# A selective-scan kernel on one core: the work of two state groups put into one GpSimd product

## The chip, the cores and the metric

The kernel runs on one core of a Trainium2 chip. The core has a matrix engine (TensorE, PE in the profile), three engines for elementwise work (VectorE is DVE, ScalarE is ACT, GpSimd is POOL), and SyncE (SP), which here only issues DMAs. Each engine takes its instructions strictly in the order of its own queue and waits on semaphores for the others. The metric is the device time of one execution in microseconds; less is better.

## The reference

Layer 0 is a ConvNeXt block (7x7 depthwise convolution, norm over channels, two dense products with GELU, residual) on x of 32 x 96 x 56 x 56. Layer 1 is two Mamba blocks over the 3,136 positions of each image, then a global-pool branch, a 1x1 fusion and a batch norm with residual. The part that matters here is the selective scan of a Mamba block, with 192 inner channels and 16 states for each:

```python
dbl = xc @ xproj_w
dt = dbl[..., :DTRANK]
Bm = dbl[..., DTRANK:DTRANK + DSTATE]
Cm = dbl[..., DTRANK + DSTATE:]
delta = jax.nn.softplus(dt @ dt_w + dt_b)
A = -jnp.exp(A_log)
dA = jnp.exp(delta[..., None] * A)
dBx = delta[..., None] * Bm[:, :, None, :] * xc[..., None]
# h[t] = dA[t] * h[t-1] + dBx[t]
hstates = jax.lax.associative_scan(comb, (dA, dBx), axis=1)[1]
y = jnp.einsum('blds,bls->bld', hstates, Cm) + Dp * xc
y = y * jax.nn.silu(z)
```

## The kernel before, in words

**Set-up.** The convolution of the first 12 images, the weights and layer 0 of the first image come first (about 0.8 ms). At the end, about 0.35 ms, the batch norm is applied to stored results.

**Stages and steps.** Everything between is a sequence of 256 stages: 32 images x 4 chunks of 784 positions x 2 Mamba blocks, the two blocks taken in turn. A stage has 24 steps, numbered n = 4j + g. A step is one scan on 128 partitions: 32 channels (j = 0 to 5) by 4 states (g = 0 to 3). "Step 24" below is step 0 of the next stage.

**What a step is made of.**
- ACT writes the factor dA (`exps`, L890), into PSUM where g = 3 or j is 2 or 5, else into a "da" tile in SBUF.
- For j = 0, 1, 3, 4, PE spreads delta*xc over the four states (`spread`, L905), once for each j, and DVE multiplies it by B (`times_b`, L878): two products ahead of the scan of g = 0 and two ahead of that of g = 1. For j = 2 and 5 (`POOLED`) GpSimd makes these products (`pooled`, L915) from a copy "us" that came by DMA.
- DVE scans (`tensor_tensor_scan`, L938) into a ring of 4 states of 784 columns.
- GpSimd multiplies the state by C (L942) into the da tile, and PE adds the four states of a channel into the PSUM tile y (`add_up`, L975), three steps later in program order.
- When both j of a pair are added up, DVE multiplies y by silu(z) (`gate`, L956). y has one buffer, so the next pair's first matmul (L969) waits for the gate. Gates stand at steps 4 and 12, and behind step 19.

**What runs beside it.** The stage's own queue positions also carry the preparation of the next stage (`prep`), the end of the last one (`post`), half a chunk of layer 0 for a later image (`block0`) and, in 192 of the stages, one channel pair of the convolution (`conv`). The order is written out by hand: each piece has a slot number, whole part the step behind which it is put into the queues, fraction the order within it; a scheduler does not move anything. Slots that the prediction speaks of: at step 0 the last part of the input projection (`project(2, wx, ...)`, L633, 16 matmul passes of PE), at step 1 silu(xc) and the projection for z (12 passes) with silu(z) (L646), which loads an activation table before it and one behind it; the layer 0 norm `hz` on DVE ahead of step 14 and the two `hn` products ahead of step 15; convolution taps at steps 7 to 10 and 18 to 22 (L552). In step n ACT's exp of step n+1 (if it goes to PSUM) and of n+2 (if to SBUF) is queued ahead of the scan. GpSimd's u = delta*xc (L712) stands at slot 16.9, its last third at 25.2.

**Queues.** `pooled` for j = 2 stands behind steps 0, 2, 4, 6, for j = 5 behind steps 12, 14, 16, 18. All loads and stores of the stages go through SP in program order: B and C of a group in one tile "bc" (8 buffers, loaded at slots 10.2 and 13.2), delta (L742), u out and back in as "us" (L726, L733), x for two stages at once (L420).

Of the kernel before, what the change touches and what calls it, by code (L numbers as in the profile page):

```python
# [34 lines left out]
F32 = mybir.dt.float32  # L35
I32 = mybir.dt.int32
AF = mybir.ActivationFunctionType
ALU = mybir.AluOpType
# [23 lines left out]
def convnext_mamba_kernel(  # L62
# [211 lines left out]
    for i in range(2):  # L274
        d = {}
        lg, lb = column(ln_g[i], C, f"lg{i}"), column(ln_b[i], C, f"lb{i}")
        wz = const.tile([C + 1, 2 * DIN], F32, name=f"inw{i}", tag=f"inw{i}")
        norm_weights(wz, in_w[i], lg, lb)
        wx = const.tile([C + 1, 4, DIN], F32, name=f"wx{i}", tag=f"wx{i}")
        nc.gpsimd.dma_start(wx, taps[i].partition_broadcast(C + 1))  # L280
        for k in range(4):
            nc.vector.tensor_tensor(wx[:, k, :], wx[:, k, :], wz[:, 0:DIN], ALU.mult)
        d["wx"], d["wz"] = wx, wz[:, DIN : 2 * DIN]
        d["cb"] = blocks(mconv_b[i], f"cb{i}")
# [59 lines left out]
    with ExitStack() as main:  # L344
# [7 lines left out]
        def work(shape, name, bufs):  # L352

            pool, n = (pre[0], 3) if pre else (wp, bufs)
            return pool.tile(shape, F32, name=name, tag=name, bufs=n)
# [41 lines left out]
        batch_sums = {}  # L397
        xins = {}

        def block0(b, c, s):  # L400
# [16 lines left out]
            def load_x():  # L417
                if s == 0:
                    xins[b, c] = work([C, CH], "xin", 1)
                    nc.sync.dma_start(xins[b, c], x[b, :, c * CH : (c + 1) * CH])  # L420

# [35 lines left out]
            def down():  # L457
                v["ps"] = psum(2)
                nc.tensor.matmul(
                    v["ps"][0:C, 0:HC], eye, xins[b, c][:, tok(s)], start=True, stop=False  # L460
                )
                for f in range(NF):
                    nc.tensor.matmul(
                        v["ps"][0:C, 0:HC], w2_sb[:, f, :], v["gl"][:, f, :],
                        start=False, stop=(f == NF - 1),
                    )

            def residual():
                xs = xins[b, c][:, tok(s)]
                nc.scalar.activation(  # L470
                    xs, v["ps"][0:C, 0:HC], AF.Identity, bias=b2ls,
                    accum_out=batch_sums[b][:, k : k + 1],
                )
                if s == 1:
                    nc.sync.dma_start(x1_d[b][:, c * CH : (c + 1) * CH], xins.pop((b, c)))

# [110 lines left out]
        def prep(S):  # L587
# [77 lines left out]
            def dbl_out():  # L665
                v["dbl"] = wp.tile([NX, CH], F32, name="dbl", tag="dbl", bufs=1)
                for a in range(2):
                    nc.scalar.copy(v["dbl"][:, tok(a)], v["pss"][a][0:NX, 0:HC])  # L668
                v["bd"] = bcd.tile([2 * NS, CH], F32, name="bd", tag="bd")
                nc.sync.dma_start(v["bd"], v["dbl"][DTR:NX, :])  # L670
                S.bcs = []

            def load_bc(gs):
                def piece():
                    for g in gs:
                        t = wp.tile([128, 2, CH], F32, name="bc", tag="bc", bufs=8)
                        for k in range(2):
                            src = v["bd"][NS * k + 4 * g : NS * k + 4 * g + 4, :]
                            nc.sync.dma_start(
                                t[:, k, :], src.unsqueeze(0).broadcast_to([32, 4, CH])  # L680
                            )
                        S.bcs.append(t)

                return piece
# [22 lines left out]

            def product(lo, hi):
                def piece():
                    if lo == 0:  # L710
                        S.u = wp.tile([128, NQ, HC], F32, name="u", tag="u", bufs=1)
                    nc.gpsimd.tensor_tensor(  # L712
                        S.u[:, lo:hi], v["dl"][:, lo:hi], S.xc[:, lo:hi], ALU.mult
                    )

                return piece

# [42 lines left out]
            elif S is stages[3]:  # L760
# [13 lines left out]
                (t[6] + 0.2, silu("z", None)), (t[7], dbl), (t[8], dbl_out),  # L774
                (max(10.2, t[8] + 1.2), load_bc((0, 1))), (max(13.2, t[8] + 2.2), load_bc((2, 3))),
                (t[9], dt), (t[10], softplus),
                (max(16.9, t[10] + 1.5), product(0, 2)), (max(18.3, t[10] + 3.1), store_u(0)),
                (25.2, product(2, 3)), (26.3, store_u(1)),
                (max(17, t[10] + 2), load_d4(0)), (max(18, t[10] + 3), load_d4(1)),
# [66 lines left out]

        ring = wp.tile([128, NG, CH], F32, name="h", tag="h", bufs=1)
        LAG = 3
        LATE = (4, 12)

# [21 lines left out]

        def product_tile(S, j, g):
            t = S.da[j, g] = wp.tile([128, CH], F32, name="da", tag="da", bufs=11)
            return t

        def times_b(S, out, g):
            nc.vector.tensor_tensor(  # L878
                halves(out), S.u4.rearrange("p (a b) -> p a b", a=2)[:, :, 0:HC],
                halves(S.bcs[g][:, 0, :]), ALU.mult,  # L880
            )

        def exps(n):

            m, r = divmod(n, NSTEP)
            if m == len(stages):
                return
            S, j, g = stages[m], r // NG, r % NG
            e = wide(g % 2)[:, 0:CH] if in_psum(j, g) else product_tile(S, j, g)
            nc.scalar.activation(e, S.d4[j], AF.Exp, scale=S.d["A"][:, j, g : g + 1])  # L890
            S.e[j, g] = e
# [17 lines left out]

        def pooled(m, j, g):  # L910


            def piece():
                S = stages[m]
                nc.gpsimd.tensor_tensor(  # L915
                    product_tile(S, j, g), S.us[j], S.bcs[g][:, 0, :], ALU.mult
                )

            return piece

        def scan(n):
            m, r = divmod(n, NSTEP)
            S, j, g = stages[m], r // NG, r % NG
            d, c = S.d, S.c
            if r in LATE and n >= NSTEP // 3:
                gate(n - LAG - 2)
            run(n, within)
            if j not in POOLED and g < 2:
                if g == 0:
                    S.w = wide(1)[:, 0:CH]  # L930
                times_b(S, S.w, g)
                if g == 0:
                    times_b(S, product_tile(S, j, NG - 1), NG - 1)
                else:
                    times_b(S, S.u4[:, 0:CH], 2)
            da = S.da[j, g]
            db = da if in_psum(j, g) else S.u4[:, 0:CH] if g == 2 else S.w
            nc.vector.tensor_tensor_scan(  # L938
                ring[:, g, :], S.e.pop((j, g)), db, 0.0 if c == 0 else d["st"][:, j, g : g + 1],
                ALU.mult, ALU.add,  # L940
            )
            nc.gpsimd.tensor_tensor(da, ring[:, g, :], S.bcs[g][:, 1, :], ALU.mult)  # L942

        def keep_state(n):

            m, r = divmod(n, NSTEP)
            S, j, g = stages[m], r // NG, r % NG
            if g % 2 == 1 and S.c < NCH - 1:
                nc.scalar.copy(  # L949
                    S.d["st"][:, j, g - 1 : g + 1].unsqueeze(2), ring[:, g - 1 : g + 1, CH - 1 : CH]  # L950
                )
# [6 lines left out]
        def add_up(n):  # L958

            if n < 0:  # L960
                return
            m, r = divmod(n, NSTEP)
            S, j, g = stages[m], r // NG, r % NG
            q = j // 2
            if j % 2 == 0 and g == 0:
                if j == 4:
                    gate(n - 1)
                S.y = py.tile([128, 512], F32, name="y", tag="y")
                nc.tensor.matmul(  # L969
                    S.y[:, 0:HC], S.d["D"][:, q, :], S.xc[:, q, :], start=True, stop=False  # L970
                )
            da = S.da.pop((j, g))
            for a in range(2):
                r0 = 64 * a + 32 * (j % 2)
                nc.tensor.matmul(  # L975
                    S.y[r0 : r0 + 32, 0:HC], ssum, da[:, tok(a)],
                    start=False, stop=(g == NG - 1),
                )
# [18 lines left out]
        for m, S in enumerate(stages):  # L997
            if m:
                put(m, post(stages[m - 1]))
            for j in POOLED:  # L1000
                put(m, [(NG * (j - 2) + 2 * g, pooled(m, j, g)) for g in range(NG)])
            if 2 <= m < len(halfs) + 2:
# [8 lines left out]
        with tc.manual_schedule(  # L1011
# [9 lines left out]
            for n in range(end + NSTEP):  # L1021
# [9 lines left out]
                if n < end + LAG:  # L1031
                    if n % NSTEP in LATE:
                        add_up(n - LAG - 1)
                    if n % NSTEP + 1 not in LATE:
                        add_up(n - LAG)
                elif n == end + LAG:
                    gate(end - 1)
# [100 lines left out]
```

## Time and profile before

| what | value |
|---|---|
| median of 3 runs | 16963.9 us (16960.82 to 16972.59) |
| the profiled execution, its span | 16951.94 us, 16950.2 us |
| PE, DVE, ACT, POOL busy | 90%, 92%, 68%, 92% of the span |
| stages from 2,000 to 15,000 us | 208 pairs of the two u products (L712): 62.5 us a stage |
| distance of two u products between 8,000 and 8,070 us | 61.24 us (8006.49 to 8067.73) |
| granted PE clock, 2,000 to 15,000 us | 0.96 |
| DMA engines | 42% busy, 138 GB/s, 2,000 to 15,000 us |

Every row of the profile tells the number of instructions, their busy time, the mean duration of one, and the idle time of the engine just ahead of them with what ended it. Where instructions follow each other without a wait, the distance of two starts in the timeline is what one costs its queue; it is a little less than the duration, since one starts before the last has ended.

### The profile page before, as it was taken

How to read it: one execution, taken by the hardware profiler on the slowest of the kernel's cores; microseconds unless marked ns; L12 is line 12 of the kernel's file. 1: busy time of each engine (PE TensorE's matmuls, PEld its weight loads, DVE VectorE, ACT ScalarE, POOL GpSimd, SP SyncE). 2: the span in 40 equal slices, each digit the busy share in tenths (PEclk: the TensorE clock that was granted, in tenths of full speed). 3: DMA queues.
4: the chain of work that ended last, by engine and by line, in shares of the span. 5: the costliest groups of instructions: out<-in, count | busy, mean ns of one | idle time of the engine just before them, and what ended most of it. 6: DMA issues, size and time to landing. Idle time of an engine off the chain costs nothing. (4 is left out here: it accounts for less than half of the span.)

```text
span 16950.2 us, 206740 instructions
## 1 busy us (share of the span) xinstructions
PE 15327.0 (90%) x69336; PEld 5507.9 (32%) x69336; DVE 15667.8 (92%) x12351; ACT 11444.5 (68%) x18723; POOL 15657.7 (92%) x8798
## 2 busy tenths in 40 slices
PE   8899999999999999999999999999998888888881
PEld 5333333333333333333333333333332222222220
DVE  8699999999999999999999999999999999999994
ACT  1577777777777777777777777677776777676653
POOL 1699999999999999999999999999999999999991
PEclk9899999999999999999999999999999999999985
DMA  4344444444444444444444444444443433433338
GB/s 113 109 139 142 142 135 140 139 142 141 135 142 140 142 135 140 142 141 137 138 141 141 142 134 141 140 143 137 137 142 131 133 126 129 134 132 133 125 121 280
DMA packets 1303109, 2362.11 MB, mean 139 GB/s; under 512 B 516398, under 2 KB 669242, under 8 KB 1302040
## 3 DMA queue, kind: packets, MB, share of 16 engines
q1 hardware_dynamic: 1292712, 2308.46, 42.0%
q10 hardware_dynamic: 7168, 38.54, 0.6%
q8 instruction: 546, 8.95, 0.2%
q14 instruction: 523, 4.28, 0.1%
q0 software_dynamic: 2160, 1.88, 0.1%
HBM read 1945.97 MB, written 402.41 MB: 139 GB/s over the span
## 5 line engine op out<-in xcount | busy, mean ns | idle before, releaser
L942 POOL TENSOR_TENSOR da<-h,bc 128x784 f32<-128x784 f32 x6144 | 11296.0, 1864 | 428.7 <-DVE h L938 356.3
L975 PE MATMUL y<-da,ssum 128*32 128x392 f32 x24576 | 5193.2, 547 | 232.7 <-POOL da L942 229.1
L890 ACT ACTIVATE w<-d,A 128x784 f32<-128x784 f32 x3072 | 2810.9, 916 | 2442.6 <-DVE h L938 2403.6
L938 DVE TENSOR_TENSOR_SCAN h<-w,st,da 128x784 f32<-128x784 f32 x2304 | 4120.7, 1831 | 267.6 <-ACT w L890 261.5
L938 DVE TENSOR_TENSOR_SCAN h<-da,st,w 128x784 f32<-128x784 f32 x2304 | 4176.3, 1834 | 3.6 <-ACT st L949 3.2
L915 POOL TENSOR_TENSOR da<-us,bc 128x784 f32<-128x784 f32 x2048 | 3811.8, 1861 | 0.0
L878 DVE TENSOR_TENSOR w<-w,bc 128x784 f32<-128x784 f32 x3072 | 2910.6, 978 | 325.6 <-PE w L905 257.4
L890 ACT ACTIVATE da<-d,A 128x784 f32<-128x784 f32 x3072 | 2834.6, 939 | 19.0 <-DMA d<-dd 16.0
L633 PE MATMUL ps<-hn,wx 97*64 97x392 f32 x12288 | 2263.2, 503 | 11.0 <-DVE hn L621 11.0
L975 PEld LDWEIGHTS y<-da,ssum 128*32 128x32 f32 x24576 | 1079.4, 116 | 3366.9 <-issue 2015.7
L905 PE MATMUL w<-u,sel 64*128 64x392 f32 x4096 | 992.4, 560 | 555.8 <-DVE h L938 436.8
L938 DVE TENSOR_TENSOR_SCAN h<-w,da 128x784 f32<-128x784 f32 x768 | 1327.4, 1771 | 125.6 <-ACT w L890 118.0
L938 DVE TENSOR_TENSOR_SCAN h<-da,w 128x784 f32<-128x784 f32 x768 | 1345.4, 1773 | 0.0
L633 PEld LDWEIGHTS ps<-hn,wx 97*64 97x64 f32 x12288 | 797.5, 136 | 1422.4 <-issue 1113.2
L712 POOL TENSOR_TENSOR u<-dl,xc 128x784 f32<-128x784 f32 (+1 forms) x512 | 736.9, 1439 | 471.0 <-ACT dl L698 471.0
L552 PE MATMUL ps<-xpad,band 112*112 112x168 f32 (+1 forms) x5376 | 1086.6, 312 | 0.0
L552 PEld LDWEIGHTS ps<-xpad,band 112*112 112x112 f32 x5376 | 709.8, 175 | 1088.3 <-issue 972.7
L690 PE MATMUL ps<-dbl,dtw 6*64 6x392 f32 x3072 | 728.0, 536 | 310.9 <-ACT dbl L668 310.9
L878 DVE TENSOR_TENSOR da<-w,bc 128x784 f32<-128x784 f32 x1024 | 988.0, 965 | 1.0 <-DMA bc<-bd 1.0
L368 ACT ACT_TABLE_LOAD x759 | 973.8, 1283 | 14.2 <-PEq L1125 0.8
L377 ACT ACTIVATE sq<-ps 96x392 f32<-96x392 f32 x768 | 345.1, 490 | 759.9 <-PE ps L372 343.6
L969 PE MATMUL y<-xc,D 128*128 128x392 f32 x1536 | 790.3, 601 | 32.8 <-DVE z L956 32.8
(152 smaller groups left out, 14579.4 us busy)
## 6 DMA issues: line engine op xcount, KB each, us to landing
bc<-bd SPq DMA_DIRECT2D x2048, 392.0 KB, 6.5
d<-dd SPq DMA_DIRECT2D x1536, 392.0 KB, 3.6
us<-uu SPq DMA_DIRECT2D x512, 392.0 KB, 3.3
dd<-dl SPq DMA_DIRECT2D x512, 294.0 KB, 3.7
band<-band_d SPq DMA_DIRECT2D x192, 343.0 KB, 4.3
uu<-u SPq DMA_DIRECT2D x1024, 49.0 KB, 3.0
cv<-conv_d SPq DMA_DIRECT2D x256, 147.0 KB, 3.4
xin<-in_x SPq DMA_DIRECT2D x128, 294.0 KB, 3.9
```

Of the source, the lines that this page charges most:

```text
L368: nc.scalar.preload_act_table_set("natural_log_exp_and_others")
L552: nc.tensor.matmul(v["ps"][0:R2, 0 : (last - first) * W], v["band"][:, dw, :], xpad[:, first:last, dw : dw + W], start=(dw == 0), stop=(dw ...
L633: nc.tensor.matmul(v["x", q][rows(a), 0:HC], weights[:, k, 64 * q : 64 * q + 64], v["hn"][:, o : o + HC], start=(k == 0), stop=(k == last),)
L712: nc.gpsimd.tensor_tensor(S.u[:, lo:hi], v["dl"][:, lo:hi], S.xc[:, lo:hi], ALU.mult)
L878: nc.vector.tensor_tensor(halves(out), S.u4.rearrange("p (a b) -> p a b", a=2)[:, :, 0:HC], halves(S.bcs[g][:, 0, :]), ALU.mult,)
L890: nc.scalar.activation(e, S.d4[j], AF.Exp, scale=S.d["A"][:, j, g : g + 1])
L905: nc.tensor.matmul(S.u4[:, 512 * a : 512 * a + HC], sel[rows(a), j % 2, :], S.u[rows(a), j // 2, :], start=True, stop=True,)
L915: nc.gpsimd.tensor_tensor(product_tile(S, j, g), S.us[j], S.bcs[g][:, 0, :], ALU.mult)
L938: nc.vector.tensor_tensor_scan(ring[:, g, :], S.e.pop((j, g)), db, 0.0 if c == 0 else d["st"][:, j, g : g + 1], ALU.mult, ALU.add,)
L942: nc.gpsimd.tensor_tensor(da, ring[:, g, :], S.bcs[g][:, 1, :], ALU.mult)
L969: nc.tensor.matmul(S.y[:, 0:HC], S.d["D"][:, q, :], S.xc[:, q, :], start=True, stop=False)
L975: nc.tensor.matmul(S.y[r0 : r0 + 32, 0:HC], ssum, da[:, tok(a)], start=False, stop=(g == NG - 1),)
```

## The change

- The product with C is made once for two scans: one GpSimd instruction over 2 x 784 columns, queued behind the scan of odd g. The ring of states has 6 places instead of 4.
- `pooled` also makes two groups at once, with the copy "us" read twice: behind steps 1 and 5 for j = 2, behind 13 and 17 for j = 5.
- The da tiles become pairs: 6 of 2 x 784 columns instead of 11 of 784. B and C get tiles of their own, each for two groups: three B pairs and four C pairs. B and C of groups 0 and 1 are loaded at slot 10.2, C of groups 2 and 3 at 13.2, B of these at 18.3.
- `add_up` is queued for two steps at a time, at even steps (steps 0 and 1 at step 4, and so on). The gates stand ahead of steps 4, 12 and 20.
- u is one product of 1,176 columns at slot 16.9; x is loaded and stored by halves of a chunk; the constant tile of the input weights keeps the half for z alone, which costs one copy for each block in the set-up.

```diff
-            if r in LATE and n >= NSTEP // 3:
+            if r in GATES and n >= NSTEP // 3:
                 gate(n - LAG - 2)
...
-            nc.gpsimd.tensor_tensor(da, ring[:, g, :], S.bcs[g][:, 1, :], ALU.mult)
+            if g % 2 == 1:
+                k = (n - 1) % NR
+                nc.gpsimd.tensor_tensor(da, ring[:, k : k + 2, :], S.bc[1, g // 2], ALU.mult)
...
                 nc.gpsimd.tensor_tensor(
-                    product_tile(S, j, g), S.us[j], S.bcs[g][:, 0, :], ALU.mult
+                    pair(S, j, h), S.us[j].unsqueeze(1).broadcast_to([128, 2, CH]), S.bc[0, h],
+                    ALU.mult,
                 )
...
-                put(m, [(NG * (j - 2) + 2 * g, pooled(m, j, g)) for g in range(NG)])
+                put(m, [(NG * (j - 2) + 4 * h + 1, pooled(m, j, h)) for h in range(2)])
...
                 if n < end + LAG:
-                    if n % NSTEP in LATE:
+                    if (n - LAG) % 2 == 1:
                         add_up(n - LAG - 1)
-                    if n % NSTEP + 1 not in LATE:
                         add_up(n - LAG)
...
-                if j == 4:
-                    gate(n - 1)
...
-        ring = wp.tile([128, NG, CH], F32, name="h", tag="h", bufs=1)
+        NR = 6
+        ring = wp.tile([128, NR, CH], F32, name="h", tag="h", bufs=1)
         LAG = 3
-        LATE = (4, 12)
+        GATES = (4, 12, 20)
...
+        def pair(S, j, h):
+
+            if (j, h) not in S.da:
+                S.da[j, h] = wp.tile([128, 2, CH], F32, name="da", tag="da", bufs=6)
+            return S.da[j, h]
...
-                (max(10.2, t[8] + 1.2), load_bc((0, 1))), (max(13.2, t[8] + 2.2), load_bc((2, 3))),
+                (max(10.2, t[8] + 1.2), load_bc(0, 0)), (max(10.2, t[8] + 1.2), load_bc(1, 0)),
+                (max(13.2, t[8] + 2.2), load_bc(1, 1)), (max(18.3, t[8] + 2.2), load_bc(0, 1)),
                 (t[9], dt), (t[10], softplus),
-                (max(16.9, t[10] + 1.5), product(0, 2)), (max(18.3, t[10] + 3.1), store_u(0)),
-                (25.2, product(2, 3)), (26.3, store_u(1)),
+                (max(16.9, t[10] + 1.5), product), (max(18.5, t[10] + 3.1), store_u(0)),
+                (26.3, store_u(1)),
...
-                    xins[b, c] = work([C, CH], "xin", 1)
-                    nc.sync.dma_start(xins[b, c], x[b, :, c * CH : (c + 1) * CH])
+                v["xin"] = work([C, HC], "xin", 1)
+                nc.sync.dma_start(v["xin"], x[b, :, k * HC : (k + 1) * HC])
```

## The prediction

> **What bounds the kernel now.** First the page: shares of busy time, then the product with C.
>
> ```profile
> PE 15327.0 (90%) x69336; PEld 5507.9 (32%) x69336; DVE 15667.8 (92%) x12351; ACT 11444.5 (68%) x18723; POOL 15657.7 (92%) x8798
> ...
> L942 POOL TENSOR_TENSOR da<-h,bc 128x784 f32<-128x784 f32 x6144 | 11296.0, 1864 | 428.7 <-DVE h L938 356.3
> ```
>
> Three engines stand at 90% or more, so no single one is "the bound"; a stage takes 62.5 us because three queues hand work to each other. The list of waits of the whole span shows where they lose it:
>
> ```profile
> DVE h L938 <- ACT w L890: 379.5, 264, 4.6
> POOL da L942 <- DVE h L938: 356.3, 476, 20.5
> DVE w L878 <- PE w L905: 257.4, 281, 8.9
> DVE z L956 <- PE y L975: 109.6, 107, 5.0
> ```
>
> DVE waits for ACT's exp and for PE's spread, GpSimd seldom for DVE, the gate hardly ever. To see what is behind "ACT w" I took the timelines of one stage. PE:
>
> ```profile
> 8018.15 0.85 PE L975 MATMUL y<-da,ssum 128*32 128x392 f32 x4
> 8019.27 0.85 PE L975 MATMUL y<-da,ssum 128*32 128x392 f32 x4 [0.28 <-POOL da L942]
> 8020.06 2.86 PE L633 MATMUL ps<-hn,wx 97*64 97x392 f32 x16
> 8022.84 0.85 PE L975 MATMUL y<-da,ssum 128*32 128x392 f32 x4
> 8023.63 2.20 PE L633 MATMUL ps<-hn,inw 97*64 97x392 f32 x12
> 8025.76 0.85 PE L975 MATMUL y<-da,ssum 128*32 128x392 f32 x4
> ```
>
> ACT, and DVE's scan of step 3:
>
> ```profile
> 8025.87 0.50 ACT L646 ACTIVATE z<-ps 128x392 f32<-128x392 f32 x1 [0.16 <-PE ps L633]
> 8026.39 1.28 ACT L368 ACT_TABLE_LOAD   x1
> 8027.68 0.92 ACT L890 ACTIVATE w<-d,A 128x784 f32<-128x784 f32 x1
> ```
>
> ```profile
> 8028.70 1.79 DVE L938 TENSOR_TENSOR_SCAN h<-w,da 128x784 f32<-128x784 f32 x1 [1.63 <-ACT w L890]
> ```
>
> The reader is to see a chain: a GpSimd product of the stage before (step 21) lets PE add it up; only then come the 16 and the 12 passes of the projections, silu(z), a table load, the exp, and scan 3. From the end of the 12 passes (8025.76) to scan 3 it is 2.94 us.
>
> **Prices, as distances of two starts.** GpSimd: six products from 8013.76 to 8024.66, 1.817 each; 392 columns 8028.31 to 8029.29, 0.98:
>
> ```profile
> 8013.76 10.94 POOL L942 TENSOR_TENSOR da<-h,bc 128x784 f32<-128x784 f32 x6
> 8024.66 1.85 POOL L915 TENSOR_TENSOR da<-us,bc 128x784 f32<-128x784 f32 x1
> ...
> 8028.31 1.02 POOL L712 TENSOR_TENSOR u<-dl,xc 128x392 f32<-128x392 f32 x1
> 8029.29 1.85 POOL L942 TENSOR_TENSOR da<-h,bc 128x784 f32<-128x784 f32 x1
> ```
>
> (1.817 - 0.98) / 392 is 2.135 ns a column, which leaves 0.143 us fixed. So 1,568 columns take 3.49 us and 1,176 take 2.65. No row is longer than 784 columns, nor reads an operand twice; the ends are 3.35 (no fixed part) and 3.63 (two products, nothing saved). I take 3.49, from both rows.
> DVE: scan 1.76 (four in 7.16 us with a kept state, five in 8.41 without, 3 to 1), product with B 0.88, gate 0.46, `hz` 0.45, both `hn` 0.92. PE: sums of a step 0.79, of two 1.5, 16 passes 2.78, 12 passes 2.13, spread 0.86, four tap passes 0.76.
> [...] The mean durations here (1.864 and 1.028) would make the pair 3.54 and the loop below 0.5 us longer; nothing else uses them.
>
> **What goes.** GpSimd's work of a stage falls from 32 x 1.817 + 1.81 + 0.98 = 60.9 us to 16 x 3.49 + 2.65 = 58.5. DVE's stays: 24 x 1.76 + 16 x 0.88 + 3 x 0.46 + 1.37 = 59.1. Were queues all that counts, 2.4 us a stage would be gained.
>
> **What comes: coarser hand-overs.** A product now starts only after its second scan and frees both sums 3.49 us later. I follow one stage from the end T of scan 13, all in us after T.
> - GpSimd (free at T): products 12/13, pooled, 14/15, u, 16/17, pooled, 18/19, 20/21, back to back. That is 7 x 3.49 + 2.65: 18/19 end at 23.59, 20/21 at **27.08**. All their scans are earlier (scan 17 at 11.93, 21 at 19.43). The second pooled pair ends at 20.10, 0.67 after DVE wanted it for scan 22.
> - PE: the spread for step 24 is queued behind the sums of 18/19: 23.59 + 1.5 + 0.2 + 0.86 = 26.15; DVE was ready at 23.62. **New wait of 2.5.** Everything on DVE is queued behind it.
> - PE: sums of 20/21, 16 and 12 passes, then ACT as above: 27.08 + 1.5 + 2.78 + 2.13 + 2.94 = 36.43 for scan 3 of the next stage; DVE is there at 34.95. Wait 1.5, in place of today's.
> - DVE to the end of scan 5: 3 x 1.76 + 0.46 + 4 x 0.88 = 9.26, so 45.69.
> - GpSimd (its product 2/3 ends at 43.7): 4/5, pooled, 6/7: 10.47, so 56.16. The pooled pair stands between because it is queued behind step 5.
> - The gate ahead of step 12 needs the sums of 6/7; DVE ended scan 11 at 56.25, the sums at 57.66: **new wait 1.4**. The spread for step 12 is queued behind these sums and two taps: 56.16 + 1.5 + 0.76 + 0.86 = 59.28, another 1.2.
> - Two scans and four products with B: 7.04. Scan 13 ends at **66.3**, where the loop closes.
>
> The same count for the kernel before, from the end of scan 16: GpSimd 8 x 1.817 + 1.81 = 16.35; PE and ACT 0.79 + 2.78 + 0.79 + 2.13 + 2.94 = 9.43; DVE from scan 3 to 16 14 x 1.76 + 10 x 0.88 + 2 x 0.46 + 1.37 = 35.7; together 61.5. The profile has 62.5, so the loop explains the stage to 1 us. The change makes it 4.8 longer. In the 62 stages without taps it is 4.1.
>
> **The PE clock.** In the new loop PE stands idle from about 18.7 to 23.6 (after the sums of 16/17 and three taps) and from about 51.4 (after the sums of 4/5 and four taps) to 56.2. The trace shows what a slack stretch does; clock is the column after the instructions:
>
> ```profile
> 8034.00:8036.00 2.00, 2.00 (x9) 0.68 0.00 0
> 8036.00:8038.00 2.00, 2.00 (x12) 0.50 0.79 170
> 8038.00:8040.00 2.00, 2.00 (x10) 0.97 0.44 139
> ```
>
> It follows a 1.26 us gap and 12 passes of only 6 rows. It costs 2 x (0.32 + 0.50 + 0.03) = 1.7 us of PE. Two such spells can fall into the loop (behind 20/21 and behind 6/7): 0 to 3.4 a stage. I take 1.7, the middle, since both idle times are longer than that gap, but part of a spell passes while PE is idle.
> [...]
>
> **Priced at nothing.** B of groups 2/3 is loaded at slot 18.3, behind the products with B of step 17 (its buffer); the store and load of u are queued behind it on SP. It is issued by about T + 11 and lands 6.5 later (median of bc), needed at 26; each us beyond would cost 1 us a stage. A pooled pair now waits for the sums of the pair before in its buffer (8/9), which end about 8 us early. Ring: scan 10 needs product 4/5 at 49.18 and starts at 49.21, no margin, but the wait at step 12 takes up some delay. x by halves: the same bytes, one load and one store more in two stages, 0.5 us each to issue, on a queue that is mostly idle: 0 to 128 us if it were not. Two set-up copies: 0.35 each (row of L282), 0 to 1 us.
>
> **Sum.** 192 stages x (4.8 + 1.7) + 62 x (4.1 + 1.7) = 1,608 us onto the profiled 16,952: **18,560 us**, +9.4%. (That execution is 12 us under the median shown.)
>
> **Rivals.**
> - *No clock spells in the loop:* 192 x 4.8 + 62 x 4.1 = 1,176, so 18,128. *Both:* 192 x 8.2 + 62 x 7.5 = 2,039, so 18,988. For the first: DVE reaches the late spread first, so some of a spell is hidden.
> - *Faster:* PE does not sit behind the late pairs, because GpSimd is early enough. If product 18/19 ended 2.5 us and 20/21 1.5 us sooner relative to the scans, and 6/7 2.6 us sooner, all new waits vanish and GpSimd's saving counts: 254 x -2.4 = -610, 16,340. For it: GpSimd has 92% busy and today hardly waits (429 us). Against: from scan 17 on, 16/17, pooled and 18/19 are 10.5 us in a row, and PE needs 2.6 more for the spread; DVE needs 11.0 from there to step 24. That holds even when GpSimd is idle before.
> - *Half of it:* one of the two closures (step 12, or step 24 with scan 3) is slack for a reason that I do not see: 2 to 4 a stage, 17,500 to 17,900.
> - *Unchanged:* gains and waits cancel by chance.
> - *B lands late:* beyond 8 us of slack, over 19,300.
> That the change does not do what it says is excluded: the built program has one GpSimd instruction for two.
>
> **Numbers.** Forecast with its clock variants, 17,900 to 19,300: 0.74. Half of it: 0.12. Over 19,300: 0.05. Faster: 0.07. Unchanged: 0.02. Low end: pair at 3.35 in ten places of the loop (-1.4), the unexplained 1 us gone, no spells: 2.4 a stage, 17,520. High end: pair at 3.63 and both spells, 19,340. As the ends do not come together, 17,600 to 19,300. A change of 0.2% is about the least that can be told from none: faster 0.07, same 0.02, slower 0.91.
>
> **What would show it.** GpSimd busy near 81%, the product of 1,568 columns 3.5 us apart, and GpSimd idle some 7 to 9 us a stage for "DVE h"; DVE waiting for "PE w" (spread) 3 to 4 us a stage instead of 1, for "PE y" (gate) over 1; PE clock under 0.96. I am wrong if DVE's waits stay near today's 3 us a stage, or if the pair costs much other than 3.5.

## The result, and the profile after

The changed kernel takes **18473.93 us** (median of 4 runs, 18462.1 to 18500.26), beside 16968.25 for the kernel before (4 runs). The ratio is 1.089, 95% interval 1.0871 to 1.0909. The forecast was 18,560. The profiled span is 18460.4 us, that of the kernel before 16950.2; over the 254 stages of the prediction's sum that is (18460.4 - 16950.2) / 254 = 5.95 us more a stage. The distance of two u products, averaged over the stages in the middle, went from 62.5 to 68.5 us.

The page of the changed kernel, busy time and the GpSimd groups (busy us, mean ns | idle us just before them):

```profile
PE 15518.4 (84%) x69336; PEld 5742.4 (31%) x69336; DVE 15723.7 (85%) x12353; ACT 11427.6 (62%) x18723; POOL 15056.7 (82%) x4446
...
L946 POOL TENSOR_TENSOR da<-h,cp 128x1568 f32<-128x1568 f32 x3072 | 10816.3, 3539 | 2547.3 <-DVE h L940 1547.9
...
L912 POOL TENSOR_TENSOR da<-us,bp 128x1568 f32<-128x1568 f32 x1024 | 3625.1, 3540 | 0.0
```

GpSimd has half the instructions (8798 became 4446) and 601 us less to do, as the change intends. DVE's work is the same to 56 us. No engine is at 90% any more: what grew is idle time. The list of waits says whose (total us, times, longest), first for the changed kernel, then PE's wait for GpSimd in the kernel before:

```profile
PE y L980 <- POOL da L946: 1911.0, 737, 5.5
POOL da L946 <- DVE h L940: 1547.9, 519, 22.7
DVE w L875 <- PE w L902: 1196.2, 515, 8.9
DVE z L961 <- PE y L980: 642.8, 261, 8.3
DVE h L940 <- POOL da L912: 235.5, 470, 2.4
DVE h L940 <- ACT w L887: 160.1, 230, 3.3
```

```profile
PE y L975 <- POOL da L942: 229.1, 347, 2.8
```

Before, the spread cost DVE 257.4 us and the gate 109.6. Now they cost 1196.2 and 642.8, and the wait for ACT's exp has fallen from 379.5 to 160.1. PE's wait for GpSimd's products went from 229.1 to 1911.0. Summed from the trace by stage (2,000 to 15,000 us), DVE's idle time grew from 3.04 to 8.86 us: for the spread from 0.96 to 4.58, for the gate from 0.36 to 2.54, 0.90 for the pooled product is new, while ACT's share fell from 1.49 to 0.69. These 5.8 us are nearly the whole 5.95: **the loss is DVE waiting for PE**, and PE waits for GpSimd.

One stage shows the closed loop. GpSimd's timeline (start, us), from the product of scans 12 and 13 to the same product one stage later:

```profile
8004.22 3.50 POOL L946 TENSOR_TENSOR da<-h,cp 128x1568 f32<-128x1568 f32 x1 [4.97 <-DVE h L940]
8007.68 3.54 POOL L912 TENSOR_TENSOR da<-us,bp 128x1568 f32<-128x1568 f32 x1
8011.18 3.53 POOL L946 TENSOR_TENSOR da<-h,cp 128x1568 f32<-128x1568 f32 x1
8014.67 2.67 POOL L709 TENSOR_TENSOR u<-dl,xc 128x1176 f32<-128x1176 f32 x1
8017.31 3.54 POOL L946 TENSOR_TENSOR da<-h,cp 128x1568 f32<-128x1568 f32 x1
...
8072.54 3.51 POOL L946 TENSOR_TENSOR da<-h,cp 128x1568 f32<-128x1568 f32 x1 [4.88 <-DVE h L940]
```

The second and third product follow each other without a wait; their starts are 3.50 and 3.49 us ahead of the next: this is the price of 1,568 columns. Between 8014.67 and 8017.31 u takes 2.64 for 1,176. The two idle times in brackets, 4.97 and 4.88, are GpSimd waiting for scan 13 at the point where the loop closes. PE's sums for scans 18/19 and for scans 6/7:

```profile
8027.86 1.51 PE L980 MATMUL y<-da,ssum 128*32 128x392 f32 x8 [3.26 <-POOL da L946]
...
8060.64 2.83 PE L980 MATMUL y<-da,ssum 128*32 128x392 f32 x8 [3.11 <-POOL da L946]
```

The same eight matmuls, after the same kind of idle time, took 1.51 us and then 2.83. The windows around the second (the clock is the column ahead of the DMA share) say why:

```profile
8060.00:8062.00 2.00, 1.36 (x6) 0.42 (x8) 0.71 (x1) 0.08 (x1) 2.00 (x2) 0.51 1.00 226
8062.00:8064.00 2.00, 2.00 (x10) 0.70 (x6) 0.48 (x1) 0.00 (x0) 2.00 (x1) 0.64 0.86 320
```

The granted clock, as a share of full speed, is 0.51 there; at 8028 to 8030 it was 1.00. This stage is typical: counted over 170 stages of the trace (numbers 20 to 189), the sums of 6/7 ran mostly at half clock in 129 and took 2.49 us on average, the sums of 18/19 in 41 and took 1.84. On DVE's timeline stand the four largest waits of the stage:

```profile
8030.66 0.98 DVE L875 TENSOR_TENSOR w<-w,bp 128x784 f32<-128x784 f32 x1 [2.67 <-PE w L902]
8040.42 1.85 DVE L940 TENSOR_TENSOR_SCAN h<-w,st,da 128x784 f32<-128x784 f32 x1 [0.77 <-ACT w L887]
8063.52 0.57 DVE L961 TENSOR_TENSOR z<-y,z 128x392 f32<-128x392 f32 x1 [2.81 <-PE y L980]
8065.15 0.98 DVE L875 TENSOR_TENSOR w<-w,bp 128x784 f32<-128x784 f32 x1 [1.06 <-PE w L902]
```

Against the prediction's loop, with T = 8004.22 in this stage (all in us after T):

| event | predicted | measured |
|---|---|---|
| sums of 18/19 can start | 23.59 | 23.64 |
| first product with B of step 24 starts | 26.15 | 26.44 |
| sums of 20/21 can start | 27.08 | 27.12 |
| scan 3 starts | 36.43 | 36.20 |
| product 4/5 starts | 45.69 | 45.84 |
| sums of 6/7 can start | 56.16 | 56.42 |
| gate | 57.66 | 59.30 |
| first product with B of step 12 | 59.28 | 60.93 |
| scan 13 has ended, the loop closes | 66.3 | 68.32 |

Up to the sums of 6/7 no entry is off by more than 0.3 us. Then the half clock adds 1.3 (2.83 - 1.51), which stays to the end; the loop closes 2.0 late.

### The profile page after: what moved, and what is told of

Read it like the earlier page. It is cut to its first block, busy times and chain, and to the rows that moved or that the text cites. A ratio compares the mean times of both kernels' runs of the same rounds, so it can differ in the third digit from the quotient of the medians.

```text
span 18460.4 us, 201326 instructions
## 1 busy us (share of the span) xinstructions
PE 15518.4 (84%) x69336; PEld 5742.4 (31%) x69336; DVE 15723.7 (85%) x12353; ACT 11427.6 (62%) x18723; POOL 15056.7 (82%) x4446
## 4 chain that ended last, share of the span: by engine, by line
POOL 37%; PE 22%; DVE 18%; issue 16%; ACT 4%; DMA 3%; POOLq 0%; SPq 0%; DVEq 0%; ACTq 0%
POOL da L946 25%; DVE h L940 12%; POOL da L912 10%; PE y L980 8%; PE ps L631 6%; DVE w L875 5%; PE w L902 3%; POOL u L709 2%; PE ps L176 2%; ACT w L887 1%; PE ps L550 1%; DMA d<-dd 1%; ACT L370 1%; PE ps L374 1%; DMA fr<-x_d 1%
## 5 line engine op out<-in xcount | busy, mean ns | idle before, releaser
L946 POOL TENSOR_TENSOR da<-h,cp 128x1568 f32<-128x1568 f32 x3072 | 10816.3, 3539 | 2547.3 <-DVE h L940 1547.9
L980 PE MATMUL y<-da,ssum 128*32 128x392 f32 x24576 | 5367.8, 565 | 1915.1 <-POOL da L946 1911.0
L875 DVE TENSOR_TENSOR w<-w,bp 128x784 f32<-128x784 f32 x3072 | 2912.2, 978 | 1258.4 <-PE w L902 1196.2
L912 POOL TENSOR_TENSOR da<-us,bp 128x1568 f32<-128x1568 f32 x1024 | 3625.1, 3540 | 0.0
L980 PEld LDWEIGHTS y<-da,ssum 128*32 128x32 f32 x24576 | 1269.5, 118 | 5336.2 <-POOL da L946 2605.6
L563 ACT ACTIVATE sq<-ps,cb 112x168 f32<-112x168 f32 (+1 forms) x384 | 144.7, 377 | 1644.5 <-PE ps L550 1644.5
L709 POOL TENSOR_TENSOR u<-dl,xc 128x1176 f32<-128x1176 f32 x256 | 686.5, 2682 | 468.7 <-ACT dl L697 468.7
L875 DVE TENSOR_TENSOR da<-w,bp 128x784 f32<-128x784 f32 x1024 | 987.3, 964 | 1.5 <-DMA bp<-bd 1.5
L550 PE MATMUL ps<-xpad,band 112*112 112x168 f32 (+1 forms) x5376 | 983.0, 311 | 0.0
L961 DVE TENSOR_TENSOR z<-y,z 128x392 f32<-128x392 f32 x768 | 423.5, 551 | 644.0 <-PE y L980 642.8
```

The costliest lines, as they stand in the source:

```text
L550: nc.tensor.matmul(v["ps"][0:R2, 0 : (last - first) * W], v["band"][:, dw, :], xpad[:, first:last, dw : dw + W], start=(dw == 0), stop=(dw ...
L709: nc.gpsimd.tensor_tensor(S.u, v["dl"], S.xc, ALU.mult)
L875: nc.vector.tensor_tensor(halves(out), S.u4.rearrange("p (a b) -> p a b", a=2)[:, :, 0:HC], halves(S.bc[0, g // 2][:, g % 2, :]), ALU.mult,)
L912: nc.gpsimd.tensor_tensor(pair(S, j, h), S.us[j].unsqueeze(1).broadcast_to([128, 2, CH]), S.bc[0, h], ALU.mult,)
L946: nc.gpsimd.tensor_tensor(da, ring[:, k : k + 2, :], S.bc[1, g // 2], ALU.mult)
L961: nc.vector.tensor_tensor(S.z[:, q, :], S.y[:, 0:HC], S.z[:, q, :], ALU.mult)
```

## The experiments

The theory is the prediction's: hand-overs of 3.5 us in place of 1.8 close a loop through GpSimd, PE and DVE that is 4.8 us longer than before, and idle time of PE adds half-clock stretches. Rivals: the price of the pair instruction itself; sums in pairs on PE; B that lands late; no part for the clock.

| kernel | median us | kernel before, same chip | ratio, 95% interval |
|---|---|---|---|
| single_products | 17147.79 | 16962.91 | 1.011 (1.0095 to 1.0125) |
| pooled_earlier | 17735.65 | 16962.91 | 1.0457 (1.0441 to 1.0472) |
| u_in_gap | 18057.9 | 16962.91 | 1.0644 (1.0626 to 1.0662) |
| pe_filler | 18187.38 | 16962.91 | 1.0724 (1.0708 to 1.074) |
| few_pairs | 16675.9 | 16954.6 | 0.9834 (0.9819 to 0.9849) |
| wx_first | 18584.73 | 16954.6 | 1.0965 (1.0949 to 1.0982) |
| before_wx_first | 16818.87 | 16954.6 | 0.9922 (0.9907 to 0.9937) |
| before_u_whole | 17189.76 | 16954.6 | 1.0138 (1.0121 to 1.0155) |
| pe_filler_two | 18160.49 | 16954.69 | 1.0709 (1.0693 to 1.0725) |
| wx_first_filled | 18102.17 | 16954.69 | 1.0675 (1.0659 to 1.0691) |
| few_pairs_wx | 16699.87 | 16954.69 | 0.9848 (0.9832 to 0.9864) |
| wx_first_filled_w1 | 17999.9 | 16954.14 | 1.0612 (1.0594 to 1.063) |

### single_products: the changed kernel with one C product for each scan

```diff
-            if g % 2 == 1:
-                k = (n - 1) % NR
-                nc.gpsimd.tensor_tensor(da, ring[:, k : k + 2, :], S.bc[1, g // 2], ALU.mult)
+            nc.gpsimd.tensor_tensor(
+                da[:, g % 2, :], state(n), S.bc[1, g // 2][:, g % 2, :], ALU.mult
+            )
```

> The changed kernel with one thing undone: the product with C is again one instruction over 784 columns behind each scan (24 a stage). Everything else stays paired: the products with B, the B, C and da tiles, the sums queued for two steps at a time, u in one piece, six states. Hand-over theory (the loop of the prediction): the second product of a pair now ends 1.82 instead of 3.49 us behind its scan, so from the end of scan 17 to the spread of step 24 it is 1.82 + 3.49 + 2 x 1.82 + 2.56 = 11.5 us against DVE's 11.0, and from scan 5 to the spread of step 12 1.82 + 3.49 + 2 x 1.82 + 3.12 = 12.1 against 11.5. Most of the new waits go: 63 to 64.5 us a stage, 17,050 to 17,450 us, although GpSimd's work grows by 1.7 us a stage. Rival, sums in pairs (PE stalls because two steps are queued at once): that is kept here, so the time stays within 200 us of 18,474. Rival, late B: kept as well, same.

It takes 17147.79 us, inside the expected range. One statement gives back 1,326 of the 1,511 us, and makes GpSimd do more. The sums on PE are still in pairs, B is still loaded late, x still by halves; so these rivals fall as main causes. In its list of waits the spread has halved, though it is still over twice the 257.4 of the kernel before, and the gate is back at its old value:

```profile
DVE w L875 <- PE w L902: 602.6, 499, 9.0
DVE z L961 <- PE y L980: 104.3, 103, 6.3
```

### pooled_earlier: another order, the same instructions

```diff
-                put(m, [(NG * (j - 2) + 4 * h + 1, pooled(m, j, h)) for h in range(2)])
+                put(m, [(NG * (j - 2) + 2 * h + 1, pooled(m, j, h)) for h in range(2)])
```

The second pooled pair stands behind step 3 (15) instead of 5 (17), so that it no longer lies between the products 4/5 and 6/7 (16/17 and 18/19).

> The changed kernel with the same instructions; only the second product with B of j = 2 and of j = 5 moves forward in GpSimd's queue, from behind steps 5 and 17 to behind steps 3 and 15. Hand-over theory: the run of GpSimd between scan 5 and the sums of 6/7 is 6.98 instead of 10.47 us, so the gate's wait ahead of step 12 (2.8 us) and the spread's behind it (1.1) all but go; the run that ends in step 24 keeps its length. 2 to 3.3 us a stage less: 17,630 to 17,970 us. Rival, the long instruction itself is what costs (price, port): nothing about it changes, 18,474 within 100 us.

It takes 17735.65 us, inside the expected range: 738 less with not one instruction more or fewer. So for this half of the loss the price of the instruction isn't the cause; its place is. Its DVE timeline shows which of the two closures went:

```profile
8023.36 0.57 DVE L961 TENSOR_TENSOR z<-y,z 128x392 f32<-128x392 f32 x1 [0.23 <-PE y L980]
...
8060.96 0.98 DVE L875 TENSOR_TENSOR w<-w,bp 128x784 f32<-128x784 f32 x1 [4.86 <-PE w L902]
```

The gate waits 0.23 us instead of 2.81 (in the whole span 195.9 instead of 642.8). The spread of step 24 still comes late, and now DVE, which gets there sooner, waits longer for it.

### u_in_gap: u moved off the way to step 24

u is cut into two thirds at slot 11.9 and one third at 25.2, in two tiles, instead of one product at 16.9.

```diff
-                (max(16.9, t[10] + 1.5), product), (max(18.5, t[10] + 3.1), store_u(0)),
+                (max(11.9, t[10] + 1.5), product(0, 2)), (25.2, product(2, 3)), (max(18.5, t[10] + 3.1), store_u(0)),
...
```

> The changed kernel with u = delta*xc in two tiles: the first two thirds move to behind step 11, where GpSimd stands idle 3 to 5 us for scan 13, the last third to the next stage's step 1. GpSimd's work grows by 0.14 us a stage. Hand-over theory: u leaves the run from scan 13 on, but the run from scan 17 on (product, pooled, two products) stays, and GpSimd only waits for scan 17 instead: 0.7 to 1.1 us a stage less, 18,190 to 18,300 us. If GpSimd's total work bound it, it would be 36 us slower; if the whole run from scan 13 counted, 2.6 us a stage less, 17,810.

It takes 18057.9 us: 416 less than the changed kernel, where 180 to 280 was expected. The direction speaks for the theory; the size is a miss, by 132 us. Part of it may be the clock: in this kernel's trace the sums of 6/7 took 1.68 us on average instead of 2.49, those of 18/19 2.10 instead of 1.84. That is 0.55 us a stage, or 140 us if all of it reaches the loop; no run tested it.

### pe_filler: more work for PE

```diff
-            pieces = [(7.5, project), (9, move(0)), (10, move(1))]
+            def filler():
+                for _ in range(10):
+                    nc.tensor.matmul(
+                        v["ps"][0][0:C, 400:512], center_m, w1_sb[0:C, 0:112],
+                        start=True, stop=True,
+                    )
+
+            pieces = [(7.5, project), (9, move(0)), (9.7, filler), (10, move(1))]
```

The added matmuls fall into the idle time ahead of the sums of 6/7; nobody reads them.

> The changed kernel with ten needless matmuls of 112 columns (20 passes, 2 to 3 us of PE) queued on PE behind step 9, into unused columns of a PSUM tile, where PE stands idle 3 to 5 us ahead of the sums of steps 6 and 7. Clock theory: the sums of 6/7 took 2.83 instead of 1.51 us, at half clock after the idle time; with PE kept at work the clock stays up, the gate's wait falls by up to 1.3 us a stage: 18,140 to 18,400 us, faster with more work. Without an effect of the clock: 18,474 within 60 us, or slower by whatever of the filler does not fit into the idle time.

It takes 18187.38 us: **287 less, with more work**. PE's timeline in this kernel shows the filler, the sums of 6/7, then the sums of 18/19:

```profile
8004.30 2.08 PE L835 MATMUL ps<-w_sb,center_m 96*96 96x112 f32 x20
8007.72 1.51 PE L987 MATMUL y<-da,ssum 128*32 128x392 f32 x8 [1.35 <-POOL da L953]
...
8041.88 2.83 PE L987 MATMUL y<-da,ssum 128*32 128x392 f32 x8 [3.20 <-POOL da L953]
```

The sums of 6/7 are at full clock. But those of 18/19, at 1.51 us in the changed kernel's stage above, are now at half: the slow stretch has partly moved to the other idle time, and DVE waits 5.01 us for the spread of step 24 in this stage instead of 2.67. Over the same 170 stages the sums of 6/7 ran mostly at half clock in 7 instead of 129, those of 18/19 in 68 instead of 41. Half-clock time in a stage with taps, summed from the trace's clock, fell from 8.0 to 6.1 us (4.6 in the kernel before).

### wx_first and before_wx_first: the 16 passes earlier

```diff
-            t = (-7.6, -7.5, -6.5, -6, 0, 0.1, 1, 2.3, 3.1, 3.4, 4)
+            t = (-7.6, -7.5, -6.5, -6, -0.8, -0.7, 1, 2.3, 3.1, 3.4, 4)
```

The same edit in both kernels puts the 16 passes of the input projection ahead of the sums that they stood behind. The passes should then no longer wait for the last product of the stage, 20/21 (21 in the kernel before).

> The changed kernel with one move on PE: the 16 passes of the projection for the next stage (slots 0.1 and 0.2) go ahead of the sums of steps 20 and 21, behind the spread of step 24. Hand-over theory: scan 3 no longer waits for product 20/21, only step 24's spread does: 0.7 to 1.2 us a stage less, 18,170 to 18,300 us. If scan 3 were held by ACT's own work (table loads), nothing changes: 18,474 within 60 us.

> The kernel before with the same move of the 16 passes. By the count of its loop the wait at scan 3 (its largest) goes, and GpSimd's own 60.9 us a stage becomes the bound: 0.5 to 0.9 us a stage less, 16,730 to 16,830 us. If that wait is only where GpSimd's limit shows, no change: 16,963 within 40 us.

In the kernel before it gains 136 us, as expected. In the changed kernel it loses 111: a clear miss. PE's timeline of wx_first shows where:

```profile
8035.37 2.83 PE L980 MATMUL y<-da,ssum 128*32 128x392 f32 x8 [3.26 <-POOL da L946]
...
8040.38 4.74 PE L631 MATMUL ps<-hn,wx 97*64 97x392 f32 x16
```

The sums of 18/19 follow 3.26 us of idle time, to the hundredth as in the changed kernel's stage, where they took 1.51. Here they take 2.83, and the 16 passes 4.74 instead of 2.86, as the slow stretch goes on. It is no single case: over 170 stages the sums of 18/19 ran mostly at half clock in 78, in the changed kernel in 41, and the passes took 3.48 us on average instead of 2.86. Half-clock time is 9.0 us a stage with taps. Yet the idle time ahead of these sums is no longer, 3.10 us on average beside 3.17: its length alone doesn't settle whether a slow stretch follows.

### Three runs with idle time filled in two places

pe_filler_two adds a second filler of ten matmuls at slot 21.7, ahead of the sums of 18/19; wx_first_filled has the earlier 16 passes as well. In both, the second filler writes to unused columns of the PSUM tile that holds the exp of step 22 at that point.

```diff
...
+        def filler():
+            for _ in range(10):
+                nc.tensor.matmul(
+                    latest[0][0:C, 912:1024], center_m, w1_sb[0:C, 0:112], start=True, stop=True
+                )
...
+            put(m, [(21.7, filler)])
```

> The changed kernel with needless PE work in both idle places of the loop: the ten matmuls behind step 9 as in pe_filler, and ten more behind step 21, ahead of the sums of 18/19. Clock theory: the stage comes down to the loop at full clock, 66.3 to 66.7 us, from 68.5: 17,920 to 18,050 us, 130 to 270 under pe_filler. Without an effect of the clock there: as pe_filler, 18,187, or slower.

> wx_first with the same needless work in both places. In wx_first the stages ran from 66.0 to 72.4 us, and the 16 passes took 4.74 us right behind PE's idle time instead of 2.86. Clock theory: that is why it was 110 us slower than the changed kernel; with PE kept at work scan 3's wait goes and the stage is 65.4 to 66.2 us: 17,700 to 17,900 us, 100 to 300 under pe_filler_two. If the move itself costs (its place in PE's queue), it stays over pe_filler_two.

pe_filler_two takes 18160.49 us, only 27 less than with one filler: inconclusive, since the experiment has a flaw. The sums of 18/19 do take 1.51 us in its timeline and half-clock time is down to 5.3 us a stage with taps, but scan 22 reads the tile that the filler writes, and waits some 2.9 us for it (670.4 us in 245 waits in its list). wx_first_filled takes 18102.17, above the expected 17,900, with the same flaw. The 16 passes are back at 2.86 us.

wx_first_filled_w1 is wx_first_filled with the filler in the other tile:

```diff
-                    latest[0][0:C, 912:1024], center_m, w1_sb[0:C, 0:112], start=True, stop=True
+                    latest[1][0:C, 912:1024], center_m, w1_sb[0:C, 0:112], start=True, stop=True
```

> wx_first_filled with one flaw mended: the needless matmuls behind step 21 wrote into the PSUM tile from which scan 22 reads its exp, so scan 22 waited for them (2.9 us a stage). They now go to the other tile, that of step 21, and only the exp of step 23 is behind them. Clock theory: with both idle places filled and the 16 passes ahead of the sums of 20/21 the stage is 65.4 to 66.3 us, 17,700 to 17,920 us. If the move of the passes costs by its place in the queue, or the clock was not the reason, it stays at 18,102 or over.

It takes 17999.9 us, 80 over the range: the filler now holds up the exp of step 23, and scan 23 waits 1.27 us in the stage looked at. Still, it is 585 us under wx_first with 20 matmuls a stage more. The cleanest comparison is that of the two kernels with the same flaw: with the idle times filled the earlier passes gain 58 us (18102.17 beside 18160.49), without fillers they cost 111. So the move's place in PE's queue is not what made wx_first slow; its loss goes with the idle times and the slow stretches behind them. In wx_first_filled_w1 the sums of 6/7 and 18/19 took 1.51 us on average and ran mostly at half clock in none of 170 stages, though half-clock time is still 7.8 us a stage with taps: it now falls elsewhere, for instance on the sums of steps 0 to 3 (4.75 us for 16 matmuls in the stage looked at). So its total alone does not tell the time: pe_filler_two has 5.3 us and takes 161 us more. What the move is worth in the changed kernel at full clock stays open, as each filler had a cost of its own.

### before_u_whole: u in one piece in the kernel before

```diff
-                (max(16.9, t[10] + 1.5), product(0, 2)), (max(18.3, t[10] + 3.1), store_u(0)),
-                (25.2, product(2, 3)), (26.3, store_u(1)),
+                (max(16.9, t[10] + 1.5), product(0, 3)), (max(18.3, t[10] + 3.1), store_u(0)),
+                (26.3, store_u(1)),
```

> The kernel before with one part of the change alone: u as one product of 1,176 columns at slot 16.9. GpSimd saves 0.14 us a stage in all, but 0.84 us more stand in its run from scan 16 to product 21. Hand-over theory: 0.5 to 0.84 us a stage more, 17,090 to 17,180 us. If GpSimd's total counted: 36 us faster.

It takes 17189.76 us, 235 more than the kernel before, 10 above the expected range. The instruction saves GpSimd 0.14 us a stage and costs 0.93. This small part of the change alone is a loss: 2.65 - 1.82 = 0.83 us more ahead of the products that PE waits for. In its list of waits DVE's wait for ACT's exp has grown from 379.5 to 506.4 us, PE's for GpSimd's products from 229.1 to 422.0, and the scans now wait 188.6 us for these products (3.9 before).

### few_pairs and few_pairs_wx: pairs only where there is time

Scans 0, 1, 6, 7, 20 and 21 get a product each again, with their sums queued singly; the other 18 stay in pairs. The pooled pairs stand behind steps 1, 3, 12 and 14, and "us" for j = 5 is loaded earlier. None of these moves was run alone in this form, so the gain belongs to them together.

```diff
...
+        SINGLE = (0, 1, 6, 7, 20, 21)
...
-            if g % 2 == 1:
+            if r in SINGLE:
+                nc.gpsimd.tensor_tensor(
+                    da[:, g % 2, :], state(n), S.bc[1, g // 2][:, g % 2, :], ALU.mult
+                )
+            elif g % 2 == 1:
...
-                put(m, [(NG * (j - 2) + 4 * h + 1, pooled(m, j, h)) for h in range(2)])
+                put(m, [((1, 3, 12, 14)[j // 5 * 2 + h], pooled(m, j, h)) for h in range(2)])
...
```

> The changed kernel with hand-overs made short only where the loop runs: the product with C is single (784 columns) for steps 0, 1, 6, 7, 20 and 21 and paired for the other 18, each single step's sums are queued alone as in the kernel before, and the four products with B stand behind steps 1, 3, 12 and 14 (the load of us for j = 5 at slot 28.6 instead of 32.9). Hand-over theory, by the same count of the loop: no new wait of a us is left, GpSimd's work is 58.9 us and DVE's 59.1, so about 60 us a stage and the 1 us that the count lacks: 61 to 61.8, 16,570 to 16,790 us, under the kernel before. If pairs as such cost time (price of the long instruction, a second read of us, the tiles), three quarters of them are still here and it stays near or over single_products, 17,150.

It takes 16675.9 us, **1.7% less than the kernel before**, the fastest of all, and inside the expected range. A stage is 61.4 us. Its page:

```profile
PE 15244.5 (92%) x69336; PEld 5654.3 (34%) x69336; DVE 15652.7 (94%) x12353; ACT 11429.9 (69%) x18723; POOL 15162.0 (91%) x5214
```

and its list of waits:

```profile
DVE w L877 <- PE w L904: 242.9, 253, 9.0
DVE z L967 <- PE y L986: 168.1, 180, 6.7
```

DVE is at 94%. The wait for the spread is back under the 257.4 of the kernel before, the gate's is a little over its 109.6. GpSimd keeps 496 of the 601 us that the full change saved it, and now that saving is of use: DVE's idle time is 1.94 us a stage, under the 3.04 of the kernel before.

few_pairs_wx adds the earlier 16 passes, and takes scans 18 and 19 out of the pairs as well:

```diff
-            t = (-7.6, -7.5, -6.5, -6, 0, 0.1, 1, 2.3, 3.1, 3.4, 4)
+            t = (-7.6, -7.5, -6.5, -6, -0.8, -0.7, 1, 2.3, 3.1, 3.4, 4)
...
-        SINGLE = (0, 1, 6, 7, 20, 21)
+        SINGLE = (0, 1, 6, 7, 18, 19, 20, 21)
```

> few_pairs with two moves more: steps 18 and 19 single too, and the 16 passes of the projection ahead of the sums of 20/21. By the count of the loop no wait is left that the move can take (GpSimd 59.2 us, DVE 59.1 a stage), so within 100 us of few_pairs' 16,676; if the scan 3 wait still ends its loop, as it did in the kernel before, 130 us or so faster.

It takes 16699.87 us: nothing further is gained.

## Why the prediction was right, step by step

- **Prices.** 3.49 us for 1,568 columns and 2.65 for 1,176, worked out from 784 and 392: measured 3.49 to 3.50 and 2.64. Reading "us" twice cost nothing here (3540 ns beside 3539). Right.
- **The loop of 66.3 us.** The table above has the events in place, and the shortest stage in the middle of the run is 66.64 us. single_products and pooled_earlier confirm it by experiment: without the coarse hand-over of the product with C 1,326 of the 1,511 us are gone; with one pooled pair moved out of each of the loop's two runs, half of them. Right.
- **Wait for the spread of step 24, 2.5 us:** 2.67 in the stage shown. **For scan 3, 1.5:** 0.77, mis-sized by half, since DVE came 0.5 later and the chain over PE and ACT ended 0.2 sooner. **For scan 22, 0.67:** 0.64 in the same stage. **For the spread of step 12, 1.2:** 1.06.
- **The gate ahead of step 12, 1.4 us, and the clock, 1.7.** They are one row in the trace: 2.81. pe_filler shows by experiment that some 287 / 254 = 1.1 us a stage hang on the idle time ahead of 6/7 and its slow stretch. The lengths of the sums agree: beside 1.51 us at full clock, those of 6/7 averaged 2.49 and those of 18/19 1.84, together 1.3 more. So the term was near, but as the middle of 0 and 3.4 it was partly luck. The prediction took PE's idle times as 4.9 and 4.8 us; in the stage shown they are 3.26 and 3.11, since other passes stand in PE's queue there. The rival with both spells in every stage did not show: the sums of 18/19 ran mostly at half clock in 41 of 170 stages, those of 6/7 in 129.
- **62.5 + 4.8 + 1.7 = 69.0 a stage:** 68.5. Over 192 stages 0.5 us is 96, about the 86 us between forecast and median.
- **Stages without taps 0.7 shorter:** mis-sized; late stages without them average 68.3 beside 68.5. They spend 14 us at half clock instead of 8.0, which may be what eats the difference; no run tested it.
- **GpSimd idle 7 to 9 us a stage for "DVE h":** 9.9 in all, of which the trace puts 6.1 down to "DVE h" and 2.7 to "PE ps". **DVE waiting for PE's spread 3 to 4:** 4.58; **for the gate over 1:** 2.54; **clock under 0.96:** 0.94. GpSimd busy 82% for "near 81%".
- **Priced at nothing.** Late B: the products with B waited 1.5 us for its DMA in the whole span. x by halves and the ring left no wait in the rows read. On the ring the prediction misread its own count: 49.21 is where scan 8 starts, scan 10 starts at 45.69 + 4 x 1.76 = 52.73, so the margin was 3.5 us. What had no margin was the pooled pair behind step 5, which ends at 45.69 + 2 x 3.49 = 52.67 and which scan 10 reads. There the trace has a wait that the prediction does not name, 0.27 us in the stage shown.
- **The rivals.** "Faster" needed 6/7, 18/19 and 20/21 earlier by 1.5 to 2.6 us and was put at 16,340. few_pairs made these products earlier, by single ones and by moving the pooled pairs, and came to 16,676: the condition was the right one, but it kept only 496 of the 601 us of GpSimd's saving, and other waits keep a part.

## What to carry to other kernels

Where several engines are near 90%, count a change along the closed loop of hand-overs between them, not in the work of one engine: here 2.4 us a stage less of GpSimd work came with 5.95 us more a stage. Merging two instructions saved a fixed part here (0.14 us), held the result of each half back by nearly a whole instruction (3.49 - 1.82 = 1.67 us), and let the first half wait for the second's input too. So merge where the consumer has slack, and leave single what a late consumer waits for. And a gap on PE may cost more than its length, when the work behind it runs at half clock (here 2.83 us instead of 1.51, behind a gap of 3.11); look at the clock column just behind the gap before filling or moving anything.

## What the runs showed of the hardware

- Matmuls that nobody needs made the kernel 287 us faster (pe_filler 18187.38 us beside 18473.93; interval of the ratios 1.0708 to 1.074 beside 1.0871 to 1.0909).
- In the traces of the changed kernel and of the kernel before, the PE clock changes only at multiples of one distance, called the grid here: counted from the first record, the 1,176 of the changed kernel begin within 0.03 us of multiples of 3.41333 us, the 676 of the kernel before likewise. Of the changed kernel's 588 stretches at a clock of 0.50, 439 last 3.41 us and 134 last 6.83; of the 338 of the kernel before, 217 and 111.
- Counted by windows from one grid point to the next, at full clock, between 2,000 and 15,000 us: with PE busy under 40% of the window, 199 of 199 were followed by half clock in the changed kernel and 39 of 39 in the kernel before; at 40 to 50%, 38 of 171 and 6 of 35; at 50 to 80%, 4 of 576 and 108 of 482.
- Of the changed kernel's windows at full clock that were at least half busy, 164 were followed by half clock even so; 160 of these hold at least six of the 12 passes over only 6 rows. In the kernel before it is 187 of 196.
- Ahead of the sums of 6/7 in the stage shown, the 3.11 us of idle time leave one window 26% busy, and half clock follows; ahead of 18/19, 3.26 us are split over windows of 62% and 43%, and none follows. In wx_first the sums behind the same 3.26 us took 2.83 us. What sets the clock is not shown: these are counts, and no run moved an idle time on the grid.
- GpSimd's elementwise product fits 0.14 us fixed and 2.135 ns a column at 392 and 784 columns (0.98 and 1.817 us between starts, kernel before) and at 1,176 and 1,568 (2.64 and 3.49, changed kernel), and cost no more with an operand read twice (3540 ns beside 3539).
